# A scan kernel's turn of y moved between epilogue tiles, with its head's weights and first loads reordered

## The chip, the cores and the metric

The kernel runs on one core of a Trainium2 chip. The metric is device time in microseconds (us), the median of several executions; lower is better. Engines are named as in the profile: PE is TensorE (PEld its weight loads), DVE is VectorE, ACT is ScalarE, POOL is GpSimd, SP is SyncE, which here only issues DMAs. ACTq, POOLq and SPq are the instruction streams of those engines when they issue a DMA.

## The reference

Four images of 64 x 64 positions and 96 channels go through a vision state-space block, then a linear attention and a quantized feed-forward layer. What matters here is the middle:

```python
xz = bilinear(x, W_in, s_in, b_in)            # bilinear: signs of x times signs of W
xp, z = jnp.split(xz, 2, axis=-1)
...                                           
t = conv3x3(sign(xc + move0_b), sign weights) # 192 -> 192 channels
xconv = silu(prelu(t + ...) + xc)
x_hwwh = jnp.stack([x_flat, x_tr], axis=1)    # by rows, by columns
xs = jnp.concatenate([x_hwwh, jnp.flip(x_hwwh, axis=-1)], axis=1)   # K = 4 directions
dts, Bs, Cs = ...                             # from sign(xs), by two bilinear layers
def step(h, inp):                             # over L = 4096 positions, N = 16 states, 192 channels
    ut, dt, Bt, Ct = inp
    h = jnp.exp(dt[..., None] * A[None]) * h + (dt * ut)[..., None] * Bt[:, :, None, :]
    return h, jnp.einsum('bkdn,bkn->bkd', h, Ct)
...
y = out_y[:, 0] + inv_y[:, 0] + wh_y + invwh_y    # the column directions are transposed back
y = layernorm(y) * silu(z)
return bilinear(y, W_out, s_out, b_out)
```

The output then gets a residual attention (its sums run over all positions of an image) and a feed-forward layer.

## The kernel before

**Scans.** `Scans.run` walks through 4 images x 4 directions x 4 column stretches of 1024 positions x 6 groups of 32 channels x 4 groups of 4 states: 1536 pieces, each one tile of 128 x 1024. Directions come in the order `KORD = (1, 3, 0, 2)`: the two by columns first, then the two by rows, so an image takes 384 pieces and a direction 96. For piece i, ACT computes the decay (`decay`, L1554), POOL the injection delta*u*B three pieces ahead (`inject`; the first one is on DVE), DVE the scan (`scan`), and either DVE or POOL the product with C; PE sums over states (`reduce`, L1628) and adds earlier directions' results (L1633, tiles loaded by `load_sums`, L1611). DVE and POOL operations of this stage go through `Tally`, a helper that adds up estimated work for each engine, so all of them show its line, L443. `scan` gives a product to POOL when VectorE's tally is ahead by more than 1.2 us of estimated work. The tallies' lead is cut to 8 us at each piece.

**Turn.** The two column directions leave their sum in `yd[3]`, ordered by columns. `turn(c, b)` brings it into row order for image b: 16 loads of 96 x 512 into tiles of the pool `f` (L1001), 16 transposing copies on ACT into a tile of 96 x 4096 (L1015), and two stores to `y13` (L1022). The fourth direction (k = 2) reads `y13`, so `run` does not go past the first such piece of an image before its turn is done:

```python
            if i % NQ == 1:
                while KORD[self.pieces[i][1]] == 2 and self.pieces[i][0] not in c.turned:
                    next(back)
                self.load_sums(i)
```

**Background.** `back()` is one Python generator that emits all other work of the scans' stage; after each piece one step of it is taken. For each image b it waits for `scans.done(b, 2)` (both column directions of b finished and 9 pieces more), turns b if that is not done, emits the `prologue` of image b + 2, then the epilogue of b: `sums` (8 tiles of 512 positions: norm, gate, output projection and the attention's sums, each ended by an addition to `vks`; some 16 pieces a tile), `middle`, and `last` (8 tiles, some 13 pieces each). `take` lets a tile of `sums` begin only when the fourth direction has passed it. Between `sums` and `middle` stands a check: if image b + 1 is within 20 pieces of `done`, it is turned there. After the last piece the rest of the last image's epilogue runs alone.

**Head.** Before the first scan, `run` interleaves two generators by hand: `weights` (`made`: loads and signs of all weights, their transposes, constants) and `prologue(c, 0)` (`first`, with `alone` set): channel sums, input projection (`project`, 16 pieces of work, the later 12 in the list `ahead`), the 3 x 3 convolution in 16 parts (`alone_parts`; v at L783 on DVE is the first operation behind a part's matmuls, sign `sg`, stores `xg` from POOL's queue at L730, `ut` copies on POOL), then row sums, delta's signs, B and C. `first` takes two steps for each of `made`. Instructions go to the engines in the order in which they are emitted.

The transposes of `weights` (L199, copied out at L201) and other small matmuls of it (tpw L359, tpd L375) use the PSUM banks y0 and y1, which `project` uses too. Tiles of weights lie in slabs ("slab" in the profile). All loads go through SP's queue but a few. `wdz`, `wdy` are delta's second weights, spread by 8 and 16 small DMAs (L331, L336); `sbR` scales and biases (12 DMAs, L395 to L397), `al` the A's logarithms (L400, Exp at L402, negated at L403), `anm` their copy (L405). `Later` delays stores by some steps, and sends them from SP at L462.

At the end of the head, B and C of the first half and of the second half are stored to `bcd` (L952) and delta's signs to `sgd` (L953), which are loaded again as `g` (L965), transposed (gp) and multiplied into delta (`Scans.start`, dA_s, w_s), spread by SP as `dl_s` (L1711). `first_u` loads u (L1658, L1660), `first_loads` eight broadcast tiles of B and C (`load_bc`, L1520).

Of the kernel before, what the change touches and what calls it, by code (L numbers as in the profile page):

```python
# [53 lines left out]
def hybrid_kernel(ctx: ExitStack, tc: tile.TileContext, a: dict, out: bass.AP):  # L54
# [108 lines left out]
    def weights():  # L163
# [39 lines left out]

        wi = temp("wi", [128, 3, DM], F32)
# [19 lines left out]
        wl = [temp(f"wl{o}", [128, DN], F32) for o in range(2)]  # L224
        for o in range(2):
            nc.gpsimd.memset(wl[o], 0.0)
            for kk in range(2):
                k, r0 = o + 2 * kk, 64 * kk
                nc.sync.dma_start(wl[o][r0 : r0 + 32, :], a["wl_bc"][32 * k : 32 * k + 32, :])
                nc.sync.dma_start(wl[o][r0 + 32 : r0 + 32 + NR, :], a["wl_dt"][k])  # L230
        wd = [temp(f"wd{x}", [128, NK, NR], F32) for x in range(2)]
        nc.sync.dma_start(wd[0], a["wd"][0:128])
        for r0 in (0, 64):
            nc.sync.dma_start(wd[1][r0 : r0 + 64], a["wd"][128:DN])
        wo = temp("wo", [DM, DN], F32)
        nc.sync.dma_start(wo, a["w_out"])
        small = {}
# [22 lines left out]
        nc.vector.tensor_tensor(sbx, pvx[:, :, B_X], pvx[:, :, MOVE0], ALU.add)  # L260
        wim = negmean("wim", wi, DM)
        wis = temp("wis", [128, 3, DM], BF16)
        for t in range(3):
            nc.scalar.activation(wis[:, t, :], wi[:, t, :], AF.Sign, bias=wim[:, t : t + 1])
        ps = transposed(winT, [wis[:, t, :] for t in range(3)])
        for x in range(2):
            nc.vector.tensor_copy(winB[:, 64 * x : 64 * x + 64], ps[0:DM, 128:DN], saturate=False)
        yield
        for i, cut in enumerate(cuts):
            nc.scalar.activation(cwA.rearrange("p t d -> p (t d)")[:, cut], cfa[i], AF.Sign, saturate=False)  # L270
            nc.scalar.activation(cwB[:, lines[i]], cfb[i], AF.Sign, saturate=False)
        yield

        part = temp("part", [96, 2, 2])
        for i in range(2):
            for h in range(2):
                nc.vector.tensor_reduce(part[:, h, i : i + 1], cwn[h][i], AX.X, ALU.add, apply_absolute_value=True)
            yield
        nc.vector.tensor_tensor(csc, part[:, :, 0], part[:, :, 1], ALU.add)
        nc.vector.tensor_scalar(csc, csc, 1.0 / (9 * DN), None, ALU.mult)  # L280

        nc.vector.tensor_tensor(cbias, pv[:, :, CONV_B], pv[:, :, RP0], ALU.add)
        nc.vector.tensor_tensor(acs, pv[:, :, PRELU], csc, ALU.mult)
        nc.vector.tensor_tensor(acb, pv[:, :, PRELU], cbias, ALU.mult)
        nc.vector.tensor_tensor(acb, acb, pv[:, :, B_X], ALU.add)
        nc.vector.tensor_tensor(acb, acb, pv[:, :, RP1], ALU.add)
        nc.vector.tensor_scalar(oma, pv[:, :, PRELU], -1.0, 1.0, ALU.mult, ALU.add)
        for h in range(2):
            nc.gpsimd.tensor_scalar(omad[:, h], i96, oma[:, h : h + 1], None, ALU.mult)
        yield  # L290

# [3 lines left out]
        kinds = (((0, 1), (2, None), (None, 0), (1, 2)), ((1, 0), (None, 2), (0, None), (2, 1)))  # L295
        for o in range(2):
# [5 lines left out]
            for kk in range(2):  # L302
                rows = slice(64 * kk, 64 * kk + 64)
                for x, pair in enumerate(kinds[kk]):
                    for half, j in enumerate(pair):
                        if j is not None:
                            to, src = we[rows, x, 64 * half : 64 * half + 64], sw[rows, 64 * j : 64 * j + 64]
                            if o:
                                to = we[rows, x, half::2]
                            else:  # L310
                                to, src = to.rearrange("p (e i) -> p i e", e=2), src.rearrange("p (i e) -> p i e", e=2)
                            nc.gpsimd.tensor_copy(to, src)
            yield
            yield
            transposed(wR[:, o].rearrange("p x m -> p (x m)"), [we[:, x, :] for x in range(4)])
            yield


        wdt = []
        for x, t in enumerate(wd):  # L320
            wdm = negmean(f"wdm{x}", t, NR)
            wds = temp(f"wds{x}", [128, NK, NR], BF16)
            for k in range(NK):
                nc.scalar.activation(wds[:, k, :], t[:, k, :], AF.Sign, bias=wdm[:, k : k + 1])
            wdt.append(temp(f"wdt{x}", [NR, NK * 32]))
            yield
            transposed(wdt[x].bitcast(F8), [wds[:, k, :] for k in range(NK)])
            yield
# [4 lines left out]
        for r0 in (0, 64):  # L333
            for s in range(8):
                at = r0 + NR * s
                nc.sync.dma_start(wdy.bitcast(F32)[at : at + NR, :, s, r0 // 4 : r0 // 4 + 16], two[:, :, 0:16])  # L336
        yield
        nc.vector.tensor_tensor(dbias, pvd[:, :, NK : 2 * NK], pvd[:, :, 2 * NK :], ALU.add)
# [3 lines left out]

# [3 lines left out]
        transposed(woutT.rearrange("p h m -> p (h m)"), [wos[:, 96 * h : 96 * h + 96] for h in range(2)])  # L346
        yield
        nc.vector.tensor_scalar(mean[:, 0], i96, -1.0 / DN, None, ALU.add)
        nc.vector.memset(mean[:, 1], -1.0 / DN)

# [1489 lines left out]
```

## Time and profile before

| | |
|---|---|
| median of 3 runs | 5361.95 us (5360.22 to 5364.72) |
| the profiled execution | 5356.94 us, span 5355.2 us |
| busy over the span | PE 63%, DVE 93%, ACT 67%, POOL 92% |
| first scan begins, last ends | 180.2 us, 5235.3 us |
| DMA | 1068.83 MB, mean 200 GB/s |

The span runs from the first to the last instruction of the profiled execution; a little time lies around it. In the list of 40 slices one slice is 134 us, and a digit is the busy share in tenths. In rows of windows the columns are the stretch, its length, then for each engine the busy time and the number of instructions, the granted TensorE clock, the DMA engines' busy share and GB/s. In the list of waits a row gives who waited, for whom, the total in us, how often, and the longest. In timeline rows the columns are start, duration, engine, line, operation, tile written <- tiles read, count, and in brackets how long the engine had been idle and what released it.

### The profile page before, as it was taken

The numbers are of one execution on the slowest core, as the hardware profiler recorded it, in microseconds if no ns is written. First come the engines' busy times: TensorE is split into PE (matmuls) and PEld (weight loads), VectorE is DVE, ScalarE is ACT, GpSimd is POOL, SyncE is SP. The second block draws the span as 40 slices with busy tenths as digits, with TensorE's granted clock in tenths as the row PEclk, the third lists the DMA queues.
The fourth block names the chain that finished last, engine by engine and source line by source line (L and its number), as shares of the span: only waits on it lengthen the run. The fifth ranks groups of instructions, "written<-read, shape, count | busy, mean of one in ns | idle before, by whom it ended". The sixth has DMA issues, their size and how long they took to land. (4 is left out here: it accounts for less than half of the span.)

```text
span 5355.2 us, 61897 instructions
## 1 busy us (share of the span) xinstructions
PE 3387.5 (63%) x20029; PEld 1351.6 (25%) x20029; DVE 5004.4 (93%) x3168; ACT 3606.7 (67%) x5644; POOL 4951.9 (92%) x2254
## 2 busy tenths in 40 slices
PE   7457665567645666566676556775666676664577
PEld 3212222122222222222222222222222222221223
DVE  4699999999999999999999999997999999999995
ACT  6577767687766666677777766666776666776554
POOL 4699999999999999999999999998999999999990
PEclk8667776678866877677777768776777776676788
DMA  5666666867766666766666666666666566667652
GB/s 107 189 194 197 212 189 203 260 203 211 222 195 182 205 218 203 230 208 204 216 204 193 193 207 224 195 198 222 201 204 211 189 209 202 200 190 233 217 177 65
DMA packets 605594, 1068.83 MB, mean 200 GB/s; under 512 B 219771, under 2 KB 336916, under 8 KB 603540
## 3 DMA queue, kind: packets, MB, share of 16 engines
q1 hardware_dynamic: 602884, 1063.93, 63.7%
q8 instruction: 157, 2.57, 0.2%
q14 instruction: 169, 1.38, 0.1%
q0 software_dynamic: 1536, 0.79, 0.1%
q10 hardware_dynamic: 848, 0.15, 0.0%
HBM read 829.69 MB, written 228.30 MB: 198 GB/s over the span
## 5 line engine op out<-in xcount | busy, mean ns | idle before, releaser
L443 POOL TENSOR_TENSOR w<-dl,bc 128x1024 f32<-128x1024 f32 x1524 | 3549.5, 2355 | 60.3 <-PE yp L1628 43.7
L1554 ACT ACTIVATE dA<-dl,anm 128x1024 f32<-128x1024 f32 x1524 | 1701.3, 1116 | 511.9 <-DVE w L443 319.0
L443 DVE TENSOR_TENSOR_SCAN dA<-dA,cy,w 128x1024 f32<-128x1024 f32 x726 | 1700.7, 2343 | 61.3 <-ACT dA L1554 50.1
L443 POOL TENSOR_TENSOR w<-h,bc 128x1024 f32<-128x1024 f32 x570 | 1341.4, 2353 | 100.5 <-DVE h L443 95.5
L1628 PE MATMUL yp<-w,sum 128*32 128x256 f32 x12288 | 1230.4, 500 | 157.4 <-ACT pd L1508 109.4
L443 DVE TENSOR_TENSOR w<-dA,bc 128x1024 f32<-128x1024 f32 x966 | 1183.3, 1225 | 63.8 <-DMA bc<-bcd 1.9
L443 DVE TENSOR_TENSOR_SCAN h<-dA,cy,w 128x1024 f32<-128x1024 f32 x426 | 996.8, 2340 | 3.4 <-ACT dA L1554 3.1
L1597 ACT COPY cy<-dA 128x1 f32<-128x1 f32 x723 | 114.2, 158 | 829.1 <-DVE w L443 828.1
L1628 PEld LDWEIGHTS yp<-w,sum 128*32 128x32 f32 x12288 | 320.0, 127 | 1218.4 <-issue 741.0
L443 DVE TENSOR_TENSOR_SCAN dA<-dA,w 128x1024 f32<-128x1024 f32 x240 | 547.7, 2282 | 50.8 <-ACT dA L1554 48.2
L443 DVE TENSOR_TENSOR_SCAN h<-dA,w 128x1024 f32<-128x1024 f32 x144 | 328.1, 2279 | 9.0 <-POOL w L443 8.6
L1489 PE MATMUL dps<-gT,wdz 128*128 128x64 fp8e5 x1008 | 115.5, 314 | 323.8 <-ACT ys L1642 313.8
L1502 PE MATMUL dps<-sp,ident 128*128 128x512 f32 x378 | 266.4, 793 | 73.1 <-ACT dps L1498 72.7
L1633 PE MATMUL yp<-ya,back 128*128 128x256 f32 x576 | 225.6, 511 | 0.0
L1489 PEld LDWEIGHTS <-wdz 128*128 128x128 fp8e5 x1008 | 94.5, 152 | 402.2 <-issue 401.3
L806 PE MATMUL cv<-tp,cwA 128*96 128x512 fp8e5 x432 | 160.2, 492 | 43.1 <-ACT r L838 41.8
L1597 ACT COPY cy<-h 128x1 f32<-128x1 f32 x429 | 79.9, 186 | 158.9 <-DVE h L443 158.6
L1489 PE MATMUL dps<-gT,wdy 128*128 128x64 fp8e5 x504 | 57.0, 312 | 183.1 <-ACT ys L1642 182.8
L1280 PE MATMUL kv<-wkv,tt 97*128 97x192 f32 x240 | 76.8, 491 | 136.9 <-DVE tt L443 136.9
L1494 ACT ACTIVATE pd<-dps,dbias,pvd 128x512 f32<-128x512 f32 x189 | 144.0, 762 | 20.9 <-PE dps L1489 20.6
L1143 PE MATMUL yc<-eys,mean 96*96 96x512 f32 x240 | 133.5, 708 | 35.6 <-DVE vks L443 21.4
L1633 PEld LDWEIGHTS yp<-ya,back 128*128 128x128 f32 x576 | 118.9, 238 | 119.3 <-issue 88.6
(380 smaller groups left out, 4559.2 us busy)
## 6 DMA issues: line engine op xcount, KB each, us to landing
dl<-dld SPq DMA_DIRECT2D x762, 512.0 KB
bc<-bcd SPq DMA_DIRECT2D x512, 512.0 KB
dld<-pd SPq DMA_DIRECT2D x126, 512.0 KB
yd<-ys SPq DMA_DIRECT2D x764, 64.0 KB
dld<-pd SPq DMA_DIRECT2D x126, 256.0 KB
ya<-yd SPq DMA_DIRECT2D x192, 128.0 KB
pu<-ud SPq DMA_DIRECT2D x32, 512.0 KB
pu<-utd SPq DMA_DIRECT2D x31, 512.0 KB
```

Source lines behind the costliest of these rows:

```text
L443: return getattr(self.eng, name)(out, *args, **kw)
L806: nc.tensor.matmul(ps, w[:, 96 * h : 96 * h + 96], tp[:, 8 * q + dy : 8 * q + dy + 8, dx : dx + IW], start=(w is taps[0][1]), stop=(w is t ...
L1143: self.c.nc.tensor.matmul(ps, w, x, start=(i == 0), stop=(i == len(pairs) - 1))
L1280: nc.tensor.matmul(pk[i // 2][:, i % 2], tt[:, 128 * i : 128 * i + 128], c.wkv, start=True, stop=True)
L1489: nc.tensor.matmul(pv[:, s], wd[:, k, s], gT[:, :, c0 : c0 + 16], start=(s == 0), stop=(s == 7))
L1494: nc.scalar.activation(d[:, 0], ps, AF.Abs, scale=sc, bias=bi)
L1502: nc.tensor.matmul(ps, c.ident, t, start=False, stop=True, skip_group_check=True)
L1554: c.nc.scalar.activation(t, self.dlt[i // NQ][0], AF.Exp, scale=c.anm[:, g, NQ * KORD[e] + q : NQ * KORD[e] + q + 1])
L1597: self.c.nc.scalar.copy(self.carries[g, q], h[:, CH - 1 : CH])
L1628: c.nc.tensor.matmul(y[32 * x : 32 * x + 32, g % 2, :], c.sum4, prod[:, 256 * x : 256 * x + 256], start=(q == 0), stop=(q == NQ - 1 and no ...
L1633: c.nc.tensor.matmul(y[:, g % 2, :], w, src, start=False, stop=(n == len(more) - 1))
```

## The change

1. `Epilogue.between`: if the next image's column scans are done and it isn't turned, turn it. It is called at the top of each tile's loop in `sums` (main lane only) and in `last`. The old check stays, for an image not turned yet.
2. `weights`: wl and wd (the rows' and delta's weights) are loaded first, from ACT's queue, and their signs and copies come as the second step, after four instead of six steps of `first`; their transposes come before the projections begin. `al` is loaded with the other weights, its Exp and `sbR`'s loads come earlier, `wdy`'s stores go from POOL's queue. What needs PSUM at the end (woutT, tpw, tpd) waits for `c.projected`, set when `ahead` is empty.
3. Row stage of the head: `g`'s margins are cleared at its start; in the second half delta's signs are stored first, and B and C only after the first gT is made. u and the first B and C are loaded from POOL's queue, right after the first half's stores, in another order.
4. Both tallies are set to zero when the scans begin.

```diff
@@ weights
+        wl = [temp(f"wl{o}", [128, DN], F32) for o in range(2)]
+        for o in range(2):
+            nc.gpsimd.memset(wl[o], 0.0)
+            for kk in range(2):
+                k, r0 = o + 2 * kk, 64 * kk
+                nc.scalar.dma_start(wl[o][r0 : r0 + 32, :], a["wl_bc"][32 * k : 32 * k + 32, :])
+                nc.scalar.dma_start(wl[o][r0 + 32 : r0 + 32 + NR, :], a["wl_dt"][k])
+        wd = [temp(f"wd{x}", [128, NK, NR], F32) for x in range(2)]
+        nc.scalar.dma_start(wd[0], a["wd"][0:128])
+        for r0 in (0, 64):
+            nc.scalar.dma_start(wd[1][r0 : r0 + 64], a["wd"][128:DN])
         wi = temp("wi", [128, 3, DM], F32)
...
-        wo = temp("wo", [DM, DN], F32)
+        wo, al = temp("wo", [DM, DN], F32), temp("al", [128, 2, NK * NS])
         nc.sync.dma_start(wo, a["w_out"])
+        nc.sync.dma_start(al, a["al"].rearrange("p h k s -> p h (k s)"))
...
+        for i, cut in enumerate(cuts):
+            nc.scalar.activation(cwA.rearrange("p t d -> p (t d)")[:, cut], cfa[i], AF.Sign, saturate=False)
+            nc.scalar.activation(cwB[:, lines[i]], cfb[i], AF.Sign, saturate=False)
+        wdt = [temp(f"wdt{x}", [NR, NK * 32]) for x in range(2)]
+        for x, t in enumerate(wds):
+            transposed(wdt[x].bitcast(F8), [t[:, k, :] for k in range(NK)])
+        yield
...
+            if i == 0:
+                for o in range(2):
+                    transposed(wR[:, o].rearrange("p x m -> p (x m)"), [wes[o][:, x, :] for x in range(4)])
+                yield
...
-                nc.sync.dma_start(wdy.bitcast(F32)[at : at + NR, :, s, r0 // 4 : r0 // 4 + 16], two[:, :, 0:16])
+                nc.gpsimd.dma_start(wdy.bitcast(F32)[at : at + NR, :, s, r0 // 4 : r0 // 4 + 16], two[:, :, 0:16])
...
+        while not c.projected:
+            yield
+        transposed(woutT.rearrange("p h m -> p (h m)"), [wos[:, 96 * h : 96 * h + 96] for h in range(2)])
...
@@ run
-    for _ in range(6):
+    for n in range(6):
+        if n == 4:
+            next(made)
         next(first)
...
-                if scans.done(b + 1, 2, 20):
+                if b + 1 not in c.turned and scans.done(b + 1, 2, 20):
@@ prologue
                                 next(ahead.pop(0), None)
+                                c.projected = not ahead
...
+                            rest.append((c.bcd[b][k][:, at : at + n], t[r0 : r0 + 32, :]))
...
+                    if not (fast and gh):
+                        for pair in rest:
+                            nc.sync.dma_start(*pair)
+                        rest.clear()
                     if fast and gh == 0:
                         c.first_u()
+                        c.loads_ahead()
...
-                    if fast and x:
-                        c.loads_ahead()
...
+                        for pair in rest:
+                            nc.sync.dma_start(*pair)
                         continue
@@ Epilogue
     def sums(self, ln):
...
+            if ln is self.lane:
+                yield from self.between()
...
+    def between(self):
+
+        b = self.b + 1
+        if not self.alone and b < NB and b not in self.c.turned and self.scans.done(b, 2):
+            yield from turn(self.c, b)
...
     def last(self, ln):
...
         while nxt:
+            yield from self.between()
             q, tt = nxt
@@ Scans
-    def load_bc(self, w, to, b, e, ci, q):
+    def load_bc(self, w, to, b, e, ci, q, eng=None):
...
-        c.nc.sync.dma_start(t, src.unsqueeze(0).to_broadcast([32, 4, CH]))
+        (eng or c.nc.sync).dma_start(t, src.unsqueeze(0).to_broadcast([32, 4, CH]))
...
-        nc.sync.dma_start(v[0], ud[0:128, 0:16])
+        nc.gpsimd.dma_start(v[0], ud[0:128, 0:16])
...
-        for w, to in enumerate((self.bt, self.ct)):
-            for q in range(NQ):
-                self.load_bc(w, to, 0, 0, 0, q)
+        for w, q in ((0, 0), (1, 0), (0, 1), (0, 2), (0, 3), (1, 1), (1, 2), (1, 3)):
+            self.load_bc(w, (self.bt, self.ct)[w], 0, 0, 0, q, self.c.nc.gpsimd)
...
         for _ in self.start():
             pass
+        c.vec.us = c.gps.us = 0.0
```

## The prediction

> **What bounds the kernel now.** I read the busy table first, then the 40 slices, the windows, the waits, and the timeline where they point.
>
> ```profile
> span 5355.2 us, 61897 instructions
> ...
> DVE  4699999999999999999999999997999999999995
> ...
> POOL 4699999999999999999999999998999999999990
> ```
>
> From slice 2 to 38 VectorE (93% of the span) and GpSimd (92%) are both full: the scans' 1536 pieces share them. Counting the scans in the timeline, the first starts at 180.2 us and the last ends at 5235.3, about 3.27 us a piece. Time is to be had only where both rows fall: the head (slices 0 and 1), slice 27, and the tail after 5235, which the change leaves alone. Slice 27, in 50-us windows (PE, PEld, DVE, ACT, POOL busy) and in the timeline:
>
> ```profile
> 3600.00:3650.00 50.00, 31.41 (x189) 12.10 (x188) 49.55 (x32) 30.20 (x38) 49.15 (x22) 0.69 0.66 213
> 3650.00:3700.00 50.00, 17.78 (x81) 6.67 (x82) 25.63 (x16) 28.33 (x40) 27.32 (x13) 0.53 0.74 227
> ```
> ```profile
> 3634.05 5.72 SPq L1001 DMA_DIRECT2D yt<-yd  x5
> ...
> 3670.24 7.72 ACT L1015 COPY yh<-yt 96x512 f32<-96x512 f32 x8 [8.83 <-DMA yt<-yd]
> ...
> 3678.39 0.56 SPq L1611 DMA_DIRECT2D ya<-yd  x1
> 3679.04 1.87 SPq L1611 DMA_DIRECT2D ya<-y  x1
> 3679.14 2.30 DVE L443 TENSOR_TENSOR_SCAN dA<-dA,w 128x1024 f32<-128x1024 f32 x1 [23.96 <-ACT dA L1554]
> ```
>
> This is one stall. Piece 1057 is the first that adds y13 of image 2, so run() forces the whole turn of image 2 through: its copies and their load latency stand ahead of the next decay on ScalarE, and VectorE idles 23.96 us. Piece to piece it is 26.8 us for 3.27, a loss of 23.5. The other turns lie at pieces 237-256, 592-611 and 1407-1425, spread out, with 3.24 to 3.28 us a piece around them: a spread turn costs nothing.
>
> In the head VectorE's waits from 30 to 135 us, and then from 135 to 215 us, are:
>
> ```profile
> DVE slab L403 <- ACT slab L402: 10.0, 1, 10.0
> DVE wR L201 <- PE tps L199: 8.1, 2, 6.1
> DVE slab L201 <- PE tps L199: 7.1, 2, 3.8
> ...
> DVE meanw L362 <- PE tpw L359: 3.3, 1, 3.3
> ```
> ```profile
> DVE h L443 <- POOL w L443: 8.6, 2, 6.3
> DVE w L443 <- DMA dl_s<-w_s: 8.6, 1, 8.6
> ```
>
> The first is a late load, queued behind 24 small stores and 12 small loads on SP:
>
> ```profile
> 91.48 0.35 SPq L400 DMA_DIRECT2D slab<-in_al  x1
> 93.28 0.31 ACT L402 ACTIVATE slab<-slab 128x128 f32<-128x128 f32 x1 [7.14 <-DMA slab<-in_al]
> 93.63 0.27 DVE L403 TENSOR_SCALAR slab<-slab 128x128 f32<-128x128 f32 x1 [9.98 <-ACT slab L402]
> ```
>
> The convolution has 16 parts; their first VectorE step (v, L783) starts at 36.8, 41.9, 49.1, 58.6, 62.5, 72.3, 80.1, 93.8, 97.3, 104.1, 108.1, 112.0, 117.1, 120.9, 124.4 and 128.2. Up to 93.8 most parts take 7 to 14 us; once the weights are done, 3.5 to 6.8.
>
> **What the Trainium skill says.** "Perfetto Trace Analysis", in "Tensor Engine Instruction", has ScalarE, VectorE and GpSimd as strict FIFO. The trace agrees: one Exp waiting on its load held v of the eighth part, whose matmuls were done, until 93.81. "DMA: Bandwidth & Descriptors", "Issuing engines are not separate DMA queues", says that all queues run on the same 16 engines, and another issuer saves only issue time. That bounds what the GpSimd queue can give: in the 5-us windows from 160 to 180 the DMA share is 0.99 to 1.03. The same page ("Queues, rings and completion order") has each engine take turns between queues by packets, so delta's loads on SP no longer stand behind all of B and C; no row of before shows such sharing.
>
> **The change, part by part.**
>
> *Turn.* Tiles of sums(1) end (their vks) at pieces 956, 972, 988, ... 1052. done(2, 2) holds from piece 970, so the turn starts at the boundary by 973 and, needing some 24 pieces, is over by 997, sixty ahead of 1057. It moves 16 loads and 2 stores on SP and 16 copies of 1.07 us on ScalarE: 17 us over 24 pieces, 0.7 a piece, where ScalarE is busy 31 of 50 us. Its first five loads took SP 5.72 us; behind them stand dl and bc loads issued 9 to 12 pieces ahead, some 30 us. Removed 23.5, less 1 to 2 for piling work into busy pieces (the 48 pieces holding the stall were followed by 48 at 3.21, so a little was already given back): **-22** (-24 to -18). What is late next: all later background work slips some 20 pieces, as the forced turn had used few. last(2) with the third turn ended near 1428 and now near 1448; sums(3) cannot take a tile before 1473. Nothing is late. The first and second turns stay (sums(0) ended at 589, its check at 586 or after).
>
> *Head, convolution.* wl and wd go first, 11 issues on ScalarE's queue at about 0.4 us (as their SP rows), so about 5 us; ScalarE computes nothing before 13.1, and wl, wd land by about 10. Their signs (0.9 and 1.7 us) come before 13.1, and GpSimd's 24 copies (6.1 us) by about 16. The four transposes then find y0 and y1 free, before the projections use these banks; nothing is left for L201 to wait on in the parts. al is loaded early: the 10 us go. woutT, tpw and tpd wait until the projections are over. wdy's 16 stores on GpSimd at 0.49 us (L730: 1.47 for three) are 8 us, between omad (30.6) and the first xg (41.8): hidden. SP keeps wdz, sbR, anm, some 15 us of issue, before the first ud store, not needed before 48. What then sets the pace is ScalarE (seven or eight operations a part, spaced 0.5 to 0.7) beside PE: the undisturbed parts 8 to 12 took 4.95 on the mean, 9 to 12 took 4.3. With 4.6 to 4.95 from 40.9 for the second part, the thirteenth starts at 91.5 to 95.4 instead of 117.1: 22 to 26 saved. Back go 2 to 5 for the moved tails (PE 1.6, DVE about 3.5) in the last four parts, which are short of slack, with utd stores filling the DMA engines (0.77 to 0.96 from 110 to 130). I take **-20**; bounds -27 and -5, the last if the parts turn out bound by their stores.
>
> *Head, behind the convolution.* With signs ahead of B and C on SP the g load goes out near 152 instead of 155.79: gp starts 3 us earlier than 157.65, and delta's broadcasts at 164.8 for 167.78. B and C (8 of 512 KB) start near 150.5 instead of 156.9. But the DMA engines were idle only 3.4 us in the 5-us windows from 145 to 160 (shares 1.00, 0.88, 0.44), so the 11 us from issue to landing of delta's first pair shrinks by 2 to 4, less if g meets B's packets. **-5** (-9 to +2).
>
> *Start of the scans.* The tally begins at zero instead of GpSimd being 8 us "ahead": the first seven products go to VectorE. Pieces 0 to 8 took 30.7 us, with VectorE waiting 8.6 on GpSimd; with scan 2.28 and product 1.22 it is 28: **-3** (-6 to 0).
>
> Sum: -22 - 20 - 5 - 3 = -50. The profiled execution took 5356.94 (span 5355.2 and 1.7 around it), 5.0 below the median of 5361.95: 5306.9 there, **5312** as the median.
>
> **Rivals.** A, above. B: the turn pays, the head hardly: the parts are bound by stores, or delta waits on B's packets anyway. For it: DMA shares of 0.77 to 1.00 from 105 to 150. Against it: in the slow stretch, 35 to 75, the share is mostly below 0.35. Gain 22 and 0 to 10: 5330 to 5340. C, slower: GpSimd's queue. It now writes the descriptors of eight broadcasts, and its injections stand behind them. The only price seen is 0.49 us for xg's 32 rows of 512 B. With 128 rows of 4 KB, by rows that is 2 us a load; by bytes (32 times) 15.7 us, and eight take 126 us. The eighth load is needed near 184: from 150 that leaves 4.3 us each before anything is lost, from 10.6 each the 50 us are gone, and from 12 each the kernel is over 0.2% slower; at 15.7 it ends near 5400. Against it: of the page's packets 266,624 lie between 2 and 8 KB, so a 4-KB row looks like one packet and not eight, and the skill's DMA page ("Anatomy of one DMA") has descriptor generation small. D: the turn does not run at 973, or an equal loss arises in the head: within 10 us of 5362.
>
> **How the numbers follow.** A 0.69, B 0.20, C 0.06, D 0.05. A's bounds give 5292 to 5330, B reaches 5341; the range is 5292 to 5341, leaving C and D out. 0.2% is 10.7 us, about what a measurement of this kernel tells from no change: faster 0.89, same 0.05, slower 0.06.
>
> **What would show it.** L1015 copies of image 2 near pieces 976 to 997 (some 3380 to 3460 us less the head's gain), no window at 25 us of DVE near 3650; v of the thirteenth part below 98; no wait of L403 or of tps within the parts; the first scan near 155, with GpSimd's eight bc issues at 2 us or less; the first product on VectorE. Wrong, if parts still take over 6 us with no weights between them (B), if bc issues are over 4 us (C), or if another forced turn appears.

## The result, and the profile after

| | before | after |
|---|---|---|
| median | 5361.09 us of 4 runs (5360.19 to 5364.72) | 5316.11 us of 4 runs (5315.57 to 5321.24) |
| the profiled execution, its span | 5356.94 us, 5355.2 us | 5316.33 us, 5314.4 us |
| first scan begins, last ends | 180.2 us, 5235.3 us | 159.35 us, 5194.94 us |

The ratio is 0.9917, 95% interval 0.99 to 0.9934: 45.0 us less by the medians, 40.8 by the spans of the profiled executions, of which that of before lies 4 us under its median. The forecast was 5312, range 5292 to 5341.

Lines have moved: the Tally's L443 is now L447, the turn's loads, copies and stores (L1001, L1015, L1022) are L1021, L1035, L1042, the decay is L1583, the loads of earlier sums L1640, v is L790.

The page after has the same count of instructions, and slice 27, which had the stall, is full. The head's two slices are a little fuller:

```profile
span 5314.4 us, 61897 instructions
...
DVE  5899999999999999999999999999999999999995
POOL 5799999999999999999999999999999999999990
```

In 50-us windows (busy time and count of PE, PEld, DVE, ACT, POOL; granted clock, DMA share, GB/s) the first row is the turn of image 2 at its new place, the other two are where it stood before:

```profile
3380.00:3430.00 50.00, 25.93 (x148) 8.82 (x140) 48.73 (x29) 36.15 (x56) 50.00 (x22) 0.70 0.81 260
3600.00:3650.00 50.00, 34.37 (x170) 13.31 (x168) 47.75 (x30) 29.02 (x44) 50.00 (x23) 0.73 0.70 219
3650.00:3700.00 50.00, 31.05 (x201) 14.56 (x201) 49.39 (x34) 30.02 (x51) 48.51 (x23) 0.77 0.65 203
```

The copies lie at pieces 975 to 994, counted by the scans that have begun; ScalarE carries them at 36 of 50 us while VectorE stays at 48.7. No window falls to half. The timeline at piece 1057 (start, duration, engine, line, operation):

```profile
3627.63 2.27 DVE L447 TENSOR_TENSOR_SCAN dA<-dA,w 128x1024 f32<-128x1024 f32 x1
...
3629.44 2.09 SPq L1640 DMA_DIRECT2D ya<-y  x1
...
3631.89 2.27 DVE L447 TENSOR_TENSOR_SCAN h<-dA,w 128x1024 f32<-128x1024 f32 x1
```

From scan to scan it is 4.3 us where before had 26.8, and the load of `y13` goes out between them without a wait.

In the head, VectorE's waits from 30 to 115 us (who waited, for whom, total, times, longest) no longer name `wR` or `al`:

```profile
DVE v L790 <- PE cv L751: 9.7, 5, 8.1
...
DVE woutT L201 <- PE tps L199: 1.1, 1, 1.1
DVE slab L347 <- ACT slab L346: 1.0, 1, 1.0
```

The 8.1 us of the first row stand ahead of the first part. Behind the convolution, from 115 to 195 us, delta's load is still there, at 7.5 us for 8.6, while the wait of h for GpSimd is gone:

```profile
DVE w L447 <- DMA dl_s<-w_s: 7.5, 1, 7.5
```

The account by landmarks, in us of each kernel's profiled execution:

| | before | after | difference |
|---|---|---|---|
| v of the first part of the convolution | 36.8 | 41.0 | +4.2 |
| v of the thirteenth part | 117.1 | 97.0 | -20.1 |
| v of the sixteenth part | 128.2 | 108.1 | -20.1 |
| first gp (transposes of g) | 157.65 | 134.10 | -23.6 |
| dA_s begins | 160.3 | 140.5 | -19.8 |
| scan of piece 0 | 180.2 | 159.4 | -20.8 |
| scan of piece 48 | 341.4 | 317.8 | -23.7 |
| scan of piece 1056 | 3648.8 | 3625.4 | -23.4 |
| scan of piece 1104 | 3829.3 | 3783.8 | -45.5 |
| scan of piece 1296 | 4453.5 | 4416.3 | -37.2 |
| last scan ends | 5235.3 | 5194.9 | -40.4 |

Head and turn brought 45.5 by piece 1104, and 8.3 of it went back in the next 192 pieces. The rest of the loop drifts by a few us either way from run to run. So do the head's landmarks: in the six traces whose head ran as after's does up to the first scan, its own included, this scan begins at 159.4 to 162.6, and after's is the earliest.

### The profile page after: what moved, and what is told of

Same layout as the page of the kernel before. It is cut to its first block, busy times and chain, and to the rows that moved or that the text cites. A ratio compares the mean times of both kernels' runs of the same rounds, so it can differ in the third digit from the quotient of the medians.

```text
span 5314.4 us, 61897 instructions
## 1 busy us (share of the span) xinstructions
PE 3386.0 (64%) x20029; PEld 1351.8 (25%) x20029; DVE 5008.9 (94%) x3172; ACT 3610.6 (68%) x5644; POOL 4956.9 (93%) x2277
## 3 DMA queue, kind: packets, MB, share of 16 engines
q10 hardware_dynamic: 1392, 0.29, 0.0%
## 5 line engine op out<-in xcount | busy, mean ns | idle before, releaser
L447 POOL TENSOR_TENSOR w<-dl,bc 128x1024 f32<-128x1024 f32 x1524 | 3549.5, 2356 | 48.6 <-PE yp L1657 32.2
L1583 ACT ACTIVATE dA<-dl,anm 128x1024 f32<-128x1024 f32 x1524 | 1701.0, 1116 | 508.7 <-DVE w L447 318.3
L447 DVE TENSOR_TENSOR_SCAN dA<-dA,cy,w 128x1024 f32<-128x1024 f32 x726 | 1700.7, 2343 | 58.6 <-ACT dA L1583 41.1
L447 POOL TENSOR_TENSOR w<-h,bc 128x1024 f32<-128x1024 f32 x566 | 1332.6, 2354 | 99.2 <-DVE h L447 94.3
L447 DVE TENSOR_TENSOR w<-dA,bc 128x1024 f32<-128x1024 f32 x970 | 1188.2, 1225 | 68.7 <-DMA bc<-bcd 7.7
L447 DVE TENSOR_TENSOR_SCAN h<-dA,cy,w 128x1024 f32<-128x1024 f32 x426 | 996.9, 2340 | 3.8 <-ACT dA L1583 3.4
L447 DVE TENSOR_TENSOR_SCAN dA<-dA,w 128x1024 f32<-128x1024 f32 x244 | 556.9, 2282 | 23.7 <-ACT dA L1583 22.4
L447 DVE TENSOR_TENSOR_SCAN h<-dA,w 128x1024 f32<-128x1024 f32 x140 | 319.0, 2279 | 0.3 <-ACT dA L1583 0.3
L1163 PE MATMUL sy<-eys,meanw 96*96 96x512 f32 x240 | 132.1, 683 | 35.8 <-ACT eys L1248 35.8
L1523 ACT ACTIVATE pd<-dps,dbias,pvd 128x512 f32<-128x512 f32 x189 | 144.0, 762 | 10.7 <-PE dps L1518 10.6
```

Of the source, the lines that this page charges most:

```text
L447: return getattr(self.eng, name)(out, *args, **kw)
L1163: self.c.nc.tensor.matmul(ps, w, x, start=(i == 0), stop=(i == len(pairs) - 1))
L1523: nc.scalar.activation(d[:, 0], ps, AF.Abs, scale=sc, bias=bi)
L1583: c.nc.scalar.activation(t, self.dlt[i // NQ][0], AF.Exp, scale=c.anm[:, g, NQ * KORD[e] + q : NQ * KORD[e] + q + 1])
```

## The experiments

My theory was the recorded sum, now with the two surprises of the table to explain: 8 us given back after piece 1104, and a head with the start of the scans that gained 23.7 by piece 48 where 28 had been added up. Each run's ratio is against runs of the kernel before on the same chip.

**Turn alone** (`e1_turn_only`). Before, with `between`, its two calls and the check for an image not turned yet:

```diff
-                if scans.done(b + 1, 2, 20):
+                if b + 1 not in c.turned and scans.done(b + 1, 2, 20):
...
+            if ln is self.lane:
+                yield from self.between()
...
+            yield from self.between()
```

> The kernel before with the turn part alone (between() and its two calls, the check for an image not turned). Theory: the forced turn at piece 1057 (26.8 us from piece to piece) is gone, the first scan stays at 180.2 us, and the whole gains 20 to 23 us, a ratio of 0.9957 to 0.9963. Rival: the later background work, shifted by some 20 pieces, gives 5 us or more of it back behind piece 1104 (in the changed kernel pieces 1104 to 1296 lost 8 us against before): 14 to 18 us, a ratio of 0.9966 to 0.9974.

5343.44 us for 5359.53 (0.9972, interval 0.996 to 0.9984): 16 us, not 22. The stall was gone (scans 1057 to 1058 in 2.9 us), yet pieces 1104 to 1296 took 637.4 us for 624.2. So what is given back there comes with the turn and needs none of the head's edits: 13 us here, 8 in after.

**Head alone** (`e2_head_only`). After, without those calls.

> The changed kernel without the calls of between(): the head's edits and the tallies' reset alone. Theory: the parts are independent and add up, so 23 us are gained (first scan at 159 us, 2.8 us more by piece 48) and the stall at piece 1057 is there as before: a ratio of 0.9955 to 0.9960. Rival: the parts are not independent, and a head that ends earlier moves the background against the forced turn: a stall at 1057 of other size than 26.8 us, and a gain that differs from 23 by 5 us or more.

5335.01 us (0.9956, 0.9943 to 0.9968): 24.5 us. Scans 1057 to 1058 stood 28.1 us apart, pieces 1104 to 1296 took 623.6. The parts add up to 16.1 + 24.5 = 40.6 beside 45.0. The 4.4 us between are within the scatter of such runs, and near the 5 by which those pieces differ; `e9_no_reset` below says where these come from.

**The phase of sums(2).** Its tiles end at pieces 1199, 1215, ... 1295 before and at 1216, 1232, ... 1312 after: 17 later. A tile takes 16 pieces and PE's work for delta (dps) returns every 8, so a tile keeps its place in that cycle for all eight tiles, and 17 shifts this place by one. Two kernels shift it elsewhere: `e7_phase7` adds seven empty steps right ahead of sums(2) (a slip of 24), `e10_slip16` takes one out of the turn of image 2 (a slip of 16, and all that stands between, the rest of sums(1) and last(1), comes one piece earlier too).

```diff
# e7_phase7, back()
             e = ends[b]
+            if b == 2:
+                for _ in range(7):
+                    yield
             e.open()
# e10_slip16, turn()
         yield
-        yield
+        if b != 2:
+            yield
```

> The changed kernel with seven empty steps of the background ahead of the third image's sums, so that this stage slips by 24 pieces against before and not by 17. The scans' own work of PE (delta's matmuls, the end of a sum) repeats every 8 pieces and a tile of sums takes 16, so a stage keeps its place in that cycle for all its 8 tiles. Theory: the loss behind the removed stall (pieces 1104 to 1296 took 632.5 us in the changed kernel and 637.4 with the turn alone, 624.2 before and 623.6 with the head alone) is this place: yc's matmuls now end just ahead of dps, and VectorE's pd and GpSimd wait for PE. With 24, a multiple of 8, these pieces take 623 to 626 us again and the whole gains 6 to 9 us on the changed kernel: a ratio of 0.990 to 0.9905. Rival: the loss has another cause (the third image's tiles meeting other transfers, a lower clock), and they take 630 us or more.

> The changed kernel with one empty step less in the third image's turn, so that its sums slip by 16 pieces against before and not by 17. Theory of the place in the cycle of 8: 16 is a multiple of 8 as 24 was, VectorE's wait of pd for PE in pieces 1104 to 1296 falls from 6.9 us to 2 or less, these pieces take 624 to 628 us for 632.5, and the whole gains 4 to 8 us on the changed kernel (a ratio of 0.9903 to 0.991). Rival: what helped with 24 was the longer delay itself, and with 16 the stretch stays at 631 us or more.

| | slip | pieces 1104 to 1296 | DVE pd waits for PE dps | POOL w for PE yp | whole |
|---|---|---|---|---|---|
| before | 0 | 624.2 | 0.5 | 2.2 | |
| turn alone | 17 | 637.4 | 7.6 | 12.3 | 0.9972 |
| after | 17 | 632.5 | 6.9 | 10.1 | 0.9917 (0.99 to 0.9934) |
| `e7_phase7` | 24 | 627.0 | 1.4 | 2.6 | 0.9904 (0.9887 to 0.992) |
| `e10_slip16` | 16 | 623.2 | none | 3.1 | 0.9895 (0.9881 to 0.9908) |

`e10_slip16` took 5304.03 us for 5359.37, `e7_phase7` 5310.76 for 5361.81: 10 and 6 us more off than the 45.0 of the change. The intervals of the totals overlap that of after, so the argument rests on the stretch and its waits. Two different edits of the phase both bring it back, `e10_slip16` fully, `e7_phase7` to within 3 us. The other kernels agree: at a slip of 17, with after and the turn alone, eight took from 628.7 (`e8_wr_early`) to 637.4, at 24 `e12_best` took 626.2, at 0 the two others 623.6 and 624.4.

Two cautions on the size. A later sums(2) ends behind piece 1296; up to piece 1344, where it is over in all kernels, before took 782.9 us, after 790.1, the turn alone 793.0, `e7_phase7` 783.1 and `e10_slip16` 777.7. And up to the end of the last scan, after loses 5.2 us of the 22 and the turn alone some 12. In `e10_slip16` some 5 us of its gain on after lie ahead of sums(2), in pieces 1056 to 1104 (153.1 us for 158.3), where this edit moves other work as well.

From the waits of VectorE and of GpSimd in these pieces, of the kernel after:

```profile
DVE pd L447 <- PE dps L1531: 6.9, 4, 2.4
```
```profile
POOL w L447 <- PE yp L1657: 10.1, 7, 2.6
```

and of `e10_slip16`, GpSimd's (VectorE has no row for dps):

```profile
POOL w L447 <- PE yp L1658: 3.1, 2, 2.8
```

One such collision in the timeline of the kernel after:

```profile
4200.43 6.49 PE L1163 MATMUL yc<-eys,mean 96*96 96x512 f32 x8 [1.73 <-DVE vks L447]
...
4207.42 1.13 PE L1531 MATMUL dps<-sp,ident 128*128 128x512 f32 x2
4207.67 2.36 POOL L447 TENSOR_TENSOR w<-dl,bc 128x1024 f32<-128x1024 f32 x1 [2.58 <-PE yp L1657]
4208.58 0.69 DVE L447 TENSOR_TENSOR pd<-dps,pu 128x512 f32<-128x512 f32 x1 [2.42 <-PE dps L1531]
```

and the corresponding tile of `e10_slip16`, where dps follows at 4193.43 and nobody waits:

```profile
4188.82 3.67 PE L1164 MATMUL yc<-eys,mean 96*96 96x512 f32 x8
```

Eight matmuls of the norm stand in PE's order ahead of the reduction and of dps, which both full engines need: VectorE stands 2.42 us, GpSimd 2.58. How long the eight take depends on the clock: 0.56 was granted from 4200 to 4207 in the first trace, 1.00 from 4188 to 4193 in the second. Not all tiles are hit: in these pieces of the kernel after, half of the yc matmuls took 593 ns or less, the longest 1169.

The place does not bring the low clock: over all of sums(2) a yc matmul took 744 ns on the mean in before, 796 in after, 814 in `e7_phase7` and 784 in `e10_slip16`, where the eight of a tile took up to 7.0 us and VectorE still never waited for dps in these pieces. There the eight begin one piece earlier ahead of the same pd. And at one place the loss follows the clock: `e8_wr_early`, at the slip of after, had 682 ns on the mean and took 628.7 us. So it takes both to lose the most, the place close ahead of that pd and a low clock.

**al early alone** (`e3_al_early`), in before:

```diff
+        nc.sync.dma_start(al, a["al"].rearrange("p h k s -> p h (k s)"))   # beside wo's load
...
-        nc.sync.dma_start(al, a["al"].rearrange("p h k s -> p h (k s)"))   # its old place
```

> The kernel before with one edit of the head alone: the load of al is issued with the other weights, not behind sbR's loads. Theory: the 10.0 us that VectorE waited for the Exp of al were on the head's path, since v of the eighth part stood behind it; it goes from 93.8 to 84-86 us and the first scan from 180.2 to 171-174: 6 to 9 us of the head's 21. Rival: the wait was the last of several that end together (SP's backlog of small DMAs delays the stores of u all the same), and the first scan comes at 177 us or later.

5354.22 us for 5359.53 (0.9991, 0.9983 to 0.9999). The 10.0-us stall shrank to 2.7: v of the eighth part came at 85.0 for 93.8. But v of the sixteenth came only 3.4 us earlier, and the first scan 4.9: between the two expectations. Its trace says where most of the 8.8 went: VectorE waited 5.7 us in all for earlier stores of u (4.0 in before), of it 4.12 at 110.3, and right behind, nine convolution matmuls took 4.04 us for 2.13 and the next six 2.19 for 1.46, at a granted clock of 0.50 from 112 to 116. Before had its low clock from 92 to 101, just as the stall ended. The turn alone, with the head of before untouched, had these two landmarks at 126.5 and 178.5, so al alone is worth 2 to 5 us: a single repair in this queue mostly uncovers the next delay.

**wR's transposes earlier** (`e8_wr_early`). In the kernel after they stand behind the first of two rounds of reductions over the convolution's weights (L313, on VectorE, which also copies them out); this puts them before:

```diff
         part = temp("part", [96, 2, 2])
+        for o in range(2):
+            transposed(wR[:, o].rearrange("p x m -> p (x m)"), [wes[o][:, x, :] for x in range(4)])
         for i in range(2):
...
-                for o in range(2):
-                    transposed(wR[:, o].rearrange("p x m -> p (x m)"), [wes[o][:, x, :] for x in range(4)])
```

> The changed kernel with wR's transposes (and their copies on VectorE) one step earlier, ahead of the first sums of the convolution's weights. Theory: the first projection (ix) waited 3.3 us for the copies of wR, which stood behind two reductions and two xb on VectorE; now it starts at 26 to 27 us for 29.8, and all that follows is 2 to 4 us earlier: first v at 37.5 to 39 us for 41.0, first scan at 155.5 to 157.5 for 159.3. Rival: VectorE's order only moves the wait (the reductions come later and v waits for acs and acb), and the first v stays at 40 us or more.

5313.38 us for 5361.81 (0.9912, 0.9897 to 0.9927). The wait went: the first projection (ix) came at 26.65 for 29.78, v of the first part at 39.35 for 41.03, of the thirteenth at 95.3 for 97.0. Then the lead of 1.7 us was gone, v of the sixteenth at 108.03 for 108.09, and the expected 155.5 to 157.5 for the first scan was missed, at 159.67. The same nine matmuls, of the fourteenth part, took 3.79 us from 95.6 where after has 2.12 from 97.3. The windows of `e8_wr_early` and of after, in 2-us stretches:

```profile
97.00:99.00 2.00, 2.00 (x6) 0.86 (x5) 1.44 (x2) 1.97 (x4) 0.18 (x1) 0.50 0.52 57
```
```profile
97.00:99.00 2.00, 1.88 (x9) 1.10 (x9) 1.79 (x4) 1.18 (x2) 1.06 (x1) 1.00 0.63 193
```

The clock, third from the right, was 0.50 for 1.00. So this trace lost its 1.7 us to the clock. Such a dip is there in some traces and not in others: `e10_slip16` and `e11_dl_pool`, which have the head of after in this part, show it too (0.50 for 3.4 us, from 99), and took 5.5 us from v of the thirteenth part to the fourteenth where after took 3.8. `e12_best` below, without a dip there, kept the lead.

**B and C, and g.** After, the second g load lands late and holds dA_s, which reads gT alone but stands behind its transposes (the second gp) in PE's order. In the timeline of after:

```profile
129.78 0.35 SPq L985 DMA_DIRECT2D g<-sgd  x1
130.22 1.85 SPq L1005 DMA_DIRECT2D bcd<-tbc  x4
132.27 0.52 SPq L985 DMA_DIRECT2D g<-sgd  x1
...
139.69 0.61 PE L993 MATMUL gp<-ident,g 128*128 128x128 fp8e5 x4 [4.56 <-DMA g<-sgd]
```

Issue to use is 4.3 us for the first load (gp at 134.10) and 7.4 for the second. Two causes offered themselves: the packets of B and C, which run on GpSimd's queue from 129.72, or the four 128-KB stores of `rest` that stand between the two loads on SP. Three kernels:

```diff
# e4_bc_late: the B and C loads emitted behind the second g load, still from GpSimd's queue
                         c.first_u()
-                        c.loads_ahead()
...
+                    if fast and x:
+                        c.loads_ahead()
# e5_bc_sp: the same, and issued from SP
-            self.load_bc(w, (self.bt, self.ct)[w], 0, 0, 0, q, self.c.nc.gpsimd)
+            self.load_bc(w, (self.bt, self.ct)[w], 0, 0, 0, q)
# e6_g_first: both g loads first, then loads_ahead (GpSimd), then rest
-                        c.loads_ahead()
...
+                    if fast and x == 0:
+                        for y in range(2):
+                            nc.sync.dma_start(gw[:, y, 16:64], c.sgd[b][ks[y]].rearrange("(p f) -> p f", p=128))
+                        c.loads_ahead()
...
```

> The changed kernel with the eight loads of B and C issued where they were before, behind the second load of g, still from GpSimd's queue. Theory: in the changed kernel their packets held up the second load of g (issued at 132.3, the transposes behind it waited until 139.7), which took back what the early signs had given; now that load lands within 4 us of its issue, delta's matmuls (dA_s) start at 136 to 137 us for 140.5, and the first scan comes at 155 to 157 us for 159.3. Rival: B and C come later and meet delta's broadcasts instead, so that the first scan stays at 159 us or comes later; a third: the stores of B and C ahead of g on SP's own queue hold it up, and dA_s stays at 139 to 141 us.

> The changed kernel with the eight loads of B and C issued by SP again, behind both loads of g (in the last run they stayed on GpSimd's queue, which waits for nothing of SP's, and so left at the same moment as in the changed kernel: 130.3 us for 129.7; that run moved nothing). Theory: the packets of B and C held up g; now g's second load lands within 4 us of its issue, its transposes follow the first ones within 3 us (5.6 in the changed kernel, 1.8 before), dA_s starts 28 to 30 us behind the last v (32.4 in the changed kernel) and the first scan 48 to 49 us behind it (51.3). Rival: SP's own stores of B and C ahead of g are what holds it up, and dA_s stays at 32 us; a second rival: delta's broadcasts, now behind B and C on one queue, take 13 us or more from issue to the first injection (10.0), and the first scan stays at 51 us or later.

> The changed kernel with both loads of g issued ahead of the second half's stores of B and C on SP; B and C still come from GpSimd's queue. Theory of the packets: nothing is gained, the second transposes stay 5 us behind the first and dA_s at 32 us behind the last v. Rival, SP's order: the second load no longer stands behind four stores of 128 KB, its transposes follow within 3 us of the first, dA_s comes at 28 to 30 us and the first scan at 48 to 49 us behind the last v.

`e4_bc_late` (5318.79 us, 0.992, 0.9907 to 0.9932) tells nothing on this: GpSimd's issues left at 130.30 as against 129.72, since nothing in the program makes its queue wait for SP's. Compare the other two, from v of the sixteenth part to dA_s and to the first scan:

| | to dA_s | to scan 0 | median | ratio |
|---|---|---|---|---|
| before | 32.1 | 52.0 | | |
| after | 32.4 | 51.3 | 5316.11 | 0.9917 |
| `e5_bc_sp` | 28.8 | 48.6 | 5316.92 | 0.9918 (0.9903 to 0.9933) |
| `e6_g_first` | 28.6 | 47.9 | 5316.16 | 0.9915 (0.99 to 0.993) |

In `e5_bc_sp` and in `e6_g_first` the second gp follows the first at once, waiting for the copy of the first and not for a load:

```profile
137.05 0.59 PE L994 MATMUL gp<-ident,g 128*128 128x128 fp8e5 x4 [0.82 <-ACT gT L1002]
```
```profile
137.35 0.59 PE L998 MATMUL gp<-ident,g 128*128 128x128 fp8e5 x4 [0.81 <-ACT gT L1006]
```

In these two, taking away either cause sufficed: stores ahead in SP's queue, or another queue's packets beside them. But `e12_best`, which has both g loads first as well, needed 3.3 us from the first gp to the second (1.85 in these two, 5.6 in after): its second load was out by 128.4, with none of those four stores ahead, and was waited for until 134.1. So it seems that the packets of B and C can hold it alone, and putting g first is not always enough. The 2.7 to 3.4 us are plain at the first scan: six other kernels with the row stage of after lie at 31.7 to 34.5 and 50.5 to 53.9. They do not show in the totals, which scatter by as much.

**Delta's first pair** (`e11_dl_pool`). Its two broadcasts go out at 148.01 and the first injection starts at 158.02: 10.0 us, and 11.1 in before. The second of each pair now from GpSimd's queue:

```diff
-                nc.sync.dma_start(r, w[x][32 * n : 32 * n + 32].unsqueeze(1).to_broadcast([32, 4, CH]))
+                (nc.gpsimd if x else nc.sync).dma_start(r, w[x][32 * n : 32 * n + 32].unsqueeze(1).to_broadcast([32, 4, CH]))
```

> The changed kernel with the second half (delta times u) of each of the first delta broadcasts issued from GpSimd's queue, idle then, and the first half from SP. The first pair takes 10.0 us from issue to the first injection though B and C have landed by 149.5, and took 11.1 before and 11.0 with B and C ahead of it on one queue. Theory: the broadcasts themselves, 512 KB each out of 32 partitions, are slow, whatever stands ahead; a second queue doesn't help, and the first injection stays 9 to 11 us behind the issue. Rival: the order on one queue is what costs, half and half then land together, and the first injection comes at 7 us or less.

5321.69 us for 5359.37 (0.9929, 0.9914 to 0.9944), and 13.0 us from issue to injection:

```profile
163.76 1.23 DVE L447 TENSOR_TENSOR w<-dl_s,bc 128x1024 f32<-128x1024 f32 x1 [10.57 <-DMA dl_s<-w_s]
```

The second tile came late. From 152 to 158 us the DMA engines moved 0.92 MB of SP's queue, which now held the first tile of all three pairs, and 0.02 MB of GpSimd's; from 158 to 164 they moved 1.03 MB of GpSimd's. The edit put this tile behind those of the next two pairs, so the run doesn't show what the order on one queue costs. What holds the pair in after is seen in the DMA engines' busy share and GB/s (the last two numbers of its windows):

```profile
140.00:145.00 5.00, 4.49 (x43) 4.30 (x41) 0.00 (x0) 3.97 (x7) 0.00 (x0) 0.57 0.96 331
150.00:155.00 5.00, 0.00 (x0) 0.00 (x0) 0.47 (x1) 0.00 (x0) 0.00 (x0) 0.50 0.96 158
155.00:160.00 5.00, 0.00 (x0) 0.00 (x0) 1.88 (x2) 4.59 (x7) 1.85 (x1) 0.50 0.97 188
```

The first row is mostly B and C coming in, the other two delta's broadcasts: the engines are as busy, and move about half as much. Why these transfers are slow stays open.

**The tallies** (`e9_no_reset`): after, without `c.vec.us = c.gps.us = 0.0`.

> The changed kernel with the tallies not set to zero when the scans begin. Theory: the first three products go to GpSimd as before, VectorE waits some 8 us on it within the first pieces, and from the first scan to piece 48 it is 2 to 3 us longer than the changed kernel's 158.4 us; the whole is 2 to 3 us slower, inside what the runs scatter. Rival: the tallies' start is given back within the first 48 pieces by later choices, and the stretch stays within 1 us of 158.4.

Pieces 0 to 8 took 30.8 us, as in before, for 27.1, and VectorE's wait of before is back, to the tenth of a us:

```profile
DVE h L447 <- POOL w L447: 8.6, 2, 6.3
```

Piece 0 to 48 is 161.2 us, as in before, for 158.4: 2.8. The whole was 5324.42 us (0.9935, 0.9923 to 0.9948), 8.3 over after's median. Of these 2.8 lie at the start and 4.3 in pieces 1104 to 1296 (636.8 us for 632.5). The turn alone, the other kernel at a slip of 17 without the reset, took 637.4 there, and the six with it 628.7 to 633.0. With no slip it hardly matters (624.2 before, 623.6 with the head alone). So in these traces the slip of 17 costs 13 us without the reset and 9 with it, and the reset is worth more than the start shows. How a start value still counts 1100 pieces later wasn't followed up.

**The best of these together** (`e12_best`): both g loads first, wR early, seven empty steps.

> The changed kernel with the three edits that helped together: both loads of g first, wR's transposes one step earlier, seven empty steps ahead of the third image's sums. Theory: the first scan at 155 to 158 us for 159.3 and 1104 to 1296 at 624 to 628 us for 632.5; the whole at 5306 to 5311 us, a ratio of 0.989 to 0.991, most of it from the empty steps. Rival: the head's 2 to 3 us don't reach the end, since with g first alone they were gone by piece 1056, and the whole is as with the empty steps alone, 5310 to 5312.

5302.5 us (5301.97 to 5311.95) for 5359.37: 0.9898, 0.9885 to 0.9912, 57 us off before. The first scan came at 153.78, 5.6 us ahead of after, with v of the sixteenth part at 104.4 for 108.1, so 3.7 of the 5.6 were there by the convolution's end. Pieces 1104 to 1296 took 626.2. Of the runs made this and `e10_slip16` are the fastest, and not to be told apart; a slip of 16 with the two head edits wasn't run.

## Why the prediction was right, and where not

The total was right: 5316 for 5312, and rival A, all as forecast, is nearest. But the profiled executions, in which the terms are counted, differ by 40.8 us where 50 were added up, and two of the four terms fell well short. By its terms:

- **Turn, -22.** The stall went as worked out: -22.1 between pieces 1056 and 1104, and the 17 us of copies beside the scans at pieces 975 to 994 cost nothing seen. What failed is "Nothing is late". Slips of 20 pieces were looked at for tiles that must wait (last(2) did end 1439, before sums(3) may start at 1473), and not for what stands on PE beside the scans at the new place. It costs 8 us in after and 13 with the turn alone, in pieces 1104 to 1296; a slip of 16 costs nothing. Net, the term was -14 by these pieces, -17 to the last scan's end and -16 by the turn alone, each time outside its bounds of -24 to -18. The prediction also missed that the calls in `last` move the turn of image 3, from pieces 1407 to 1425 to 1358 to 1377; pieces 1344 to 1392 took 153.9 us for 155.8, so it cost nothing there.
- **Convolution, -20.** It was -20.1, from two mis-sized terms that cancelled. The pace was right: parts 1 to 13 took 56.0 us, 4.66 each, within the 4.6 to 4.95 forecast, where before took 80.3. But the start was 4.2 us later, not equal: the 11 loads on ScalarE's queue ran from 1.55 to 11.4 us, not for 5. Their issues took 4.4 us, 0.4 each as forecast. What the sum lacked is three waits between them, 5.2 us together, which ended as loads of x landed (twice) and one of wl. So wd's signs ran past 13.1, and wR's copies did hold the projections. In the timeline of after:

```profile
2.63 0.32 ACTq L209 DMA_DIRECT2D slab<-in_wl_bc  x1
...
4.80 0.28 ACTq L210 DMA_DIRECT2D slab<-in_wl_dt  x1
...
5.18 0.32 ACTq L209 DMA_DIRECT2D slab<-in_wl_bc  x1
...
7.98 0.28 ACTq L210 DMA_DIRECT2D slab<-in_wl_dt  x1
...
13.68 1.61 ACT L288 ACTIVATE slab<-slab,slab 128x6 bf16<-128x6 f32 x8
15.20 0.45 ACT L597 COPY csr<-csum 1x384 f32<-1x384 f32 x1
...
29.78 0.39 PE L653 MATMUL ix<-xsT,winT 96*128 96x512 fp8e5 x1 [3.31 <-DVE wR L201]
```

  csr, the first step of the channel sums, came at 13.12 in before. Against it, the 2 to 5 us to be given back in the last four parts didn't come: 11.1 us in both kernels. That -20 was met to 0.1 is luck: v of the sixteenth part came at 126.5 and 128.2 in the two kernels with the head of before, and at 108.1 to 111.6 in the nine with after's head up to there, so the term is 15 to 20.
- **Behind the convolution, -5.** It was -0.7. The first gp did come 3.5 us earlier against the convolution's end, as forecast; the second came 3.8 later behind the first, since its g load was held by stores ahead of it and by B and C beside it; and delta's first pair shrank by 1.0, not by 2 to 4. The prediction had named this risk ("less if g meets B's packets") and left it to its bound of +2, out of its value. That pair did stand behind B and C in before, as the prediction said. It was issued at 167.8, and the windows of before have

```profile
170.00:175.00 5.00, 0.00 (x0) 0.00 (x0) 0.25 (x1) 0.00 (x0) 0.00 (x0) 0.50 1.03 373
175.00:180.00 5.00, 0.00 (x0) 0.00 (x0) 1.17 (x1) 4.02 (x5) 1.01 (x1) 0.50 1.01 195
```

  first at the rate of B and C's loads, then at that of such broadcasts, so the pair, used at 178.8, itself needed some 5 us (an estimate from these rows). In after B and C had landed by 149.5, and the pair still took 10.0. The wait went, and a slower transfer took its place, which the prediction's 2 to 4 didn't count.
- **Start, -3.** -2.8, and `e9_no_reset` gives the same; what the reset brought later, some 4 us at this slip, was no term of the sum.
- **Rival C** is out: five of GpSimd's issues of B and C took 2.76 us together, 0.55 each, where 10.6 were needed to lose the gain. **B** is out as well: the head alone paid 24.5 us. More was to be had from it, though: `e12_best` starts its scans 5.6 us ahead of after.

## What to carry to other kernels

A forced stall costs its whole length, so do the work as soon as its inputs are done; but then everything behind it in a hand-made order moves, and where it lands against a periodic step on a shared in-order engine can take back a quarter to a half of the gain (5 to 12 of 22 us here, counted to the end of the last scan): shift it by a step or two and look at the waits. When weights are moved to the front of a start-up, price the waits between their loads, not only the issues, and the steps they now stand ahead of. A small load that someone waits for goes ahead of the bulk on its own queue, and where that isn't enough, keep bulk off the other queues till it lands.

## What the runs showed of the hardware

- **The granted clock falls in short stretches** within a stage: 0.50 for some 4 us in the convolution, at 112 to 116 in `e3_al_early`, from 95.6 to 99.0 in `e8_wr_early`, not at all in after from 85 to 110. Nine matmuls went from 2.12 to between 3.79 and 4.04 us. Of the eleven kernels with the convolution of after, three show the dip between its thirteenth and fourteenth part. A lead of 2 us upstream can vanish there, so such a step isn't judged by one trace.
- **The place of a DMA in the program did not order it against another engine's queue**: emitted later in `e4_bc_late`, GpSimd's loads still left at the same moment (130.30 and 129.72). The Trainium skill ("DMA: Bandwidth & Descriptors", "Queues, rings and completion order") has each DMA engine take turns between queues by packets. The second g load agrees: 7.4 us from issue to use beside B and C, and at most 4.2 in `e5_bc_sp`, where these come later. `e11_dl_pool` shows no such turns: from 152 to 158 GpSimd's queue moved 0.02 MB beside SP's 0.92, though its three loads were issued by 153.3. Whether its packets were ready by then the trace doesn't show.
- **A broadcast from 32 to 128 partitions moved about half of what loads of B and C did, at the same busy share of the DMA engines**: 158 to 188 GB/s at 0.96 to 0.97 in after, beside 331 at 0.96; in before 195 at 1.01, beside 373 at 1.03. A pair of 512-KB tiles took 10.0 us from issue to use with B and C landed soon after its issue.
